# A gate left in PSUM and node one-hots made by eight comparisons, in a message-passing kernel on one core

## The chip, the core and the metric

The kernel runs on one core of a Trainium2 chip. A core has engines that run their own instruction queues side by side: TensorE (PE, with weight loads shown apart as PEld), VectorE (DVE), ScalarE (ACT), GpSimd (POOL) and SyncE (SP), and 16 DMA engines[...]. They meet through semaphores. The metric is the device time of one execution in microseconds, as the median of several runs. A separate execution is recorded by the hardware profiler, and everything that is said of single instructions comes from that one.

## What is computed

Four graph layers run over 6,250 nodes with 64 features and 206,250 edges that are sorted by their target node. The change lies in the third layer alone. Cut to what matters:

```python
h = relu(layernorm(x))
# third layer: V = h, E = edge_attr_64 (206250 x 64)
V  = leaky_relu(V, 0.2)
Vp = leaky_relu(V @ pAw + pAb, 0.2) @ pBw + pBb
e  = relu(relu(E @ mlp_w1 + mlp_b1) @ mlp_w2 + mlp_b2)
scale = sigmoid(e @ Bw + Bb)
shift = e @ Cw + Cb
msg  = scale * Vp[src] + shift
M    = clip(msg, 1e-5) ** 2
mean = segment_sum(M, dst) / max(count(dst), 1)
x    = x + sqrt(mean)
```

`scale` is called the gate below. The other three layers are sums over neighbours, which the kernel does as matmuls with a dense matrix of edge counts, A.

## The kernel before

The edges are padded to 202 groups of 1,024: 128 partitions times J = 8 edges. A loop of slots runs over the groups (`slot`, L1428 on). It is a software pipeline: slot i starts group i and works on later steps of groups i-1 to i-6. TensorE, ScalarE and VectorE run in the order in which the slot writes their instructions down, so the code's order is each engine's queue. POOL and SP are not bound to it: they run ahead as far as buffers allow.

What happens to a group:

- `loaded` brings the edge features in from HBM, started on SP.
- `fetched` (L1354) gathers the rows Vp[src] into the tile `v`, by eight indirect DMAs that POOL issues, one for each of a partition's eight edges. `v` has four buffers, so POOL can be up to four groups ahead of the instruction that reads `v`. The row numbers come from the tile `src_g`.
- `turned_edges`, `layer` and `evicted` transpose the features and apply the two small layers (PE and ACT).
- `gates_and_shifts` (L1376, L1380) makes gate and shift side by side in one PSUM tile, `p_bc`, 128 x 8 x 2 x 64. There is one such tile, so the next group's matmuls wait until this group's reader is done.
- `gated` (L1385) is the sigmoid on ScalarE.
- `clipped` (L1389 to L1391) is, on VectorE, gate times `v`, plus shift, and the maximum with 1e-5.
- `squared` (L1396, L1397) squares on ScalarE. The square goes on as three bf16 parts in `m3`, through L1452 (VectorE), L1453 (ScalarE) and L1464 (VectorE).
- `compared_nodes` (L1401) makes the one-hots `to` that say which of 128 target nodes each edge belongs to.
- `summed` (L1408) multiplies, for each of the eight edges of a partition, the one-hot by the message: eight matmuls with `to` as the weights.
- `added_to_nodes` (L1416, L1421, L1424) folds the three parts and adds them to the nodes.

Between these, the slot places pieces of two other jobs: `crossed` (L1260 on PE, L1266 on VectorE) compares blocks of A with their mirror images, and `partial` (L748, L1285) starts the last layer's sums. Both share a pair of PSUM buffers, `p_sum`. `finished` (L1323 on) runs when the last group of a column of blocks is done.

`prepared` builds what the loop needs, during an earlier stage: among it `lane` (L1124, each edge's target node modulo 128, as bf16) and `count` (L1131, 0 to 127, each repeated eight times).

Of the kernel before, what the change touches and what calls it, by code (L numbers as in the profile page):

```python
# [8 lines left out]
F32 = mybir.dt.float32  # L9
BF16 = mybir.dt.bfloat16  # L10
FP16 = mybir.dt.float16
I32 = mybir.dt.int32
AF = mybir.ActivationFunctionType
OP = mybir.AluOpType
AX = mybir.AxisListType

P = 128
N = 6250
D = 64
# [6 lines left out]
J = 8  # L26
G = -(-E // (P * J))
# [589 lines left out]
def fast(ctx, tc, bad, x, src, dst, edge_attr, W3, b3, W4, b4, w1, b1, w2, b2, Bw, Bb, Cw, Cb,  # L617
         pAw, pAb, pBw, pBb, out):

    nc = tc.nc  # L620
# [135 lines left out]
    with ExitStack() as ph:  # L756

        ipool = ph.enter_context(tc.tile_pool(name="ipool", bufs=1, reuse_waits="tile"))
        with ExitStack() as first:
# [9 lines left out]
                op0=OP.mult)  # L769
# [6 lines left out]
                                           op0=OP.mult, op1=OP.add)  # L776
# [9 lines left out]
        count = ipool.tile([P, 128, GQ], BF16, name="count")  # L786
# [14 lines left out]
        for c0, c1 in ((0, 3), (3, 10), (10, GC)):  # L801
            for c in range(c0, c1):
# [5 lines left out]
                                    op0=OP.mult, op1=OP.max)  # L808
# [21 lines left out]
        with ExitStack() as ps:  # L830
            psum = ps.enter_context(tc.tile_pool(name="ps0", bufs=1, space=PSUM, reuse_waits="tile"))
            p = psum.tile([P, SG, P], F32, name="p_a", bufs=2)
            nc.tensor.transpose(p[:D, 0, :], W3_sb, ident)
            nc.vector.tensor_copy(W3T, p[:D, 0, :])
            p = psum.tile([P, SG, P], F32, name="p_a", bufs=2)
# [34 lines left out]
            for c in range(GC):  # L870
# [6 lines left out]
                                        op0=OP.is_lt, op1=OP.add, accum_out=n)  # L877
                nc.vector.tensor_add(exact_i[:, c:c + 1], begin[:, c:c + 1], n)
            for c in range(GC):
# [6 lines left out]
                                        op0=OP.subtract)  # L886
                nc.scalar.activation(digits[:, 1, :], run[:, :, 1], AF.Copy)
                p = psum.tile([P, 1024], BF16, name="p_dig")
# [6 lines left out]
                if c % 9 == 8 or c == GC - 1:  # L895
                    c0 = c // 9 * 9
                    p = psum.tile([P, 512], F32, name="p_node")
                    for k in range(3):
# [4 lines left out]
                        for i in range(c0, c + 1):  # L903
# [11 lines left out]
                                    op=OP.add)  # L915
            by_col = ipool.tile([GC, P, 2], F32, name="by_col")
            p = psum.tile([P, 512], F32, name="p_node")
# [7 lines left out]
            p = psum.tile([P, 512], F32, name="p_node")  # L925
# [116 lines left out]
    def prepared(psum):  # L1042

        cpool = apart.enter_context(tc.tile_pool(name="cpool", bufs=1, side="right", reuse_waits="tile"))
# [35 lines left out]
        for i in range(4):  # L1080
# [5 lines left out]
            for j0 in range(0, J, 4):  # L1086
                p = psum.tile([P, 4, GH], F32, name="p_turn", bufs=2)
# [19 lines left out]
        for g in range(1, G + 1):  # L1107
            if g == G or window(g) != window(g0):
# [4 lines left out]
                                op=OP.subtract)  # L1113
# [6 lines left out]
                                op=OP.add)  # L1120
        yield

        nc.vector.tensor_scalar(dst_g, dst_g, P - 1, None, op0=OP.bitwise_and)
        lane = cpool.tile([P, G, J], BF16, name="lane")  # L1124
        nc.vector.tensor_copy(lane, dst_g)
        own = cpool.tile([P, P // QN, 2], F32, name="own")
        nc.vector.memset(own[:, :, 0], 0.0)
        for q in range(P // QN):
            nc.vector.memset(own[q * QN:(q + 1) * QN, :q + 1, 0], 1.0)
        nc.vector.tensor_scalar(own[:, :, 1], own[:, :, 0], -1.0, 1.0, op0=OP.mult, op1=OP.add)  # L1130
        count = cpool.tile([P, P, J], BF16, name="count")  # L1131
        nc.gpsimd.iota(count, pattern=[[1, P], [0, J]], base=0, channel_multiplier=0,
                       allow_small_or_imprecise_dtypes=True)

        before.close()
# [7 lines left out]
    with ExitStack() as ph:  # L1143
        wpool = ph.enter_context(tc.tile_pool(name="wpool", bufs=2, reuse_waits="tile"))
        values = []
        with tc.tile_pool(name="apool", bufs=7, reuse_waits="tile") as apool, \
                tc.tile_pool(name="ps1", bufs=1, space=PSUM, reuse_waits="tile") as psum:

            def convolved(c, z):
                add_whole(z, V3, c)  # L1150
                nc.vector.tensor_mul(z, z, over_features(norm0[:, blocks(c)]))
                nc.vector.tensor_add(z, z, over_blocks(b4_r, CB))
                nc.vector.tensor_add(X[:, blocks(c), :], X[:, blocks(c), :], z)
                h = wpool.tile([P, CB, D], F32, name="h")
                if c == 0:
                    values.append(of_nodes(node))
                normed_and_split(h, values[0], c, norm3)


            with tc.manual_schedule(engines={ET.PE, ET.DVE}):  # L1160
                gather(apool, wpool, psum, V3, convolved, (
                    step for steps in (hidden(NC - 1, wpool, psum), prepared(psum))
                    for step in steps))
# [50 lines left out]
    with ExitStack() as ph:  # L1214
        cpool, w1_d, w2_d, b1_c, b2_c, BC, BC_b, ones, src_g, lane, own, count = made.pop()
        mpool = ph.enter_context(tc.tile_pool(name="mpool", bufs=3, reuse_waits="tile"))
# [126 lines left out]
        of = [{} for _ in range(G)]  # L1343
# [37 lines left out]
                                     h2[:, q * P:(q + 1) * P], BC, start=False, stop=(k == 1))  # L1381

        def gated(g):
            gate = of[g]["gate"] = mpool.tile([P, J, D], F32, name="gate")
            nc.scalar.activation(gate, of[g]["p_bc"][:, :, 0, :], AF.Sigmoid)  # L1385

        def clipped(g):
            m = of[g]["m"] = mpool.tile([P, J, D], F32, name="m")
            nc.vector.tensor_mul(m, of[g].pop("gate"), of[g].pop("v"))  # L1389
            nc.vector.tensor_add(m, m, of[g].pop("p_bc")[:, :, 1, :])  # L1390
            nc.vector.tensor_scalar_max(m, m, EPS)  # L1391

        def squared(g):
# [3 lines left out]
            nc.scalar.activation(m, m, AF.Square)  # L1397

        def compared_nodes(g):
            to = of[g]["to"] = mpool.tile([P, P, J], BF16, name="to")  # L1400
            nc.vector.tensor_tensor(  # L1401
                to, count, lane[:, g, :].unsqueeze(1).to_broadcast([P, P, J]), op=OP.is_equal)

        def summed(g):
            p = of[g]["p_s"] = ps_a.tile([P, 512], F32, name="p_s")[:, :3 * D]
            m3, to = of[g].pop("m3"), of[g].pop("to")
            for j in range(J):
                nc.tensor.matmul(p, to[:, :, j], m3[:, j].rearrange("p t f -> p (t f)"),  # L1408
                                 start=(j == 0), stop=(j == J - 1))

        begun = set()
# [16 lines left out]
        def slot(i):  # L1428
# [7 lines left out]
            if at(M_AT):  # L1436
                gated(i - M_AT)
                clipped(i - M_AT)
# [10 lines left out]
            if at(M_AT):  # L1449
                compared_nodes(i - M_AT)  # L1450
                m, m3 = of[i - M_AT].pop("m"), of[i - M_AT]["m3"]
                nc.vector.tensor_sub(m, m, m3[:, :, 0, :])  # L1452
                nc.scalar.activation(m3[:, :, 1, :], m, AF.Copy)  # L1453
# [13 lines left out]
            if at(SUM_AT):  # L1467
                summed(i - SUM_AT)
# [28 lines left out]
    with ExitStack() as ph:  # L1497
# [5 lines left out]
        for layer in range(3):  # L1503
# [25 lines left out]
            else:  # L1529
                for s in range(CS):  # L1530
# [3 lines left out]
                    t = whole[:, :, s % 2 * CW:(s % 2 + 1) * CW]  # L1534
                    p = psum.tile([P, 512], F32, name="p_sum", bufs=2)
# [48 lines left out]
```

## Time and profile before

| what | value |
|---|---|
| timed runs, median of 3 | 4,146.01 us (4,139.06 to 4,147.82) |
| the profiled execution's own time | 3,611.97 us |
| its span, first to last instruction | 3,610.2 us |
| TensorE clock granted, mean | 0.904 |
| busy in the span: PE, PEld, DVE, ACT, POOL | 84%, 59%, 54%, 34%, 46% |
| gathers L1354, POOL | 1,616, busy 1,592.1 us |
| gate times v, L1389, DVE | 202, mean 694 ns |
| one-hots, L1401, DVE | 202, mean 687 ns |
| sigmoid, L1385, ACT | 202, mean 603 ns from 1,500 to 3,000 us |

The profile's page has the busy time of each engine, the span in slices, the chain of work that ended last, and groups of instructions by line with their mean duration and the idle time of the engine just before them. A trace can also be asked for the instructions of one line or tile, for the busy time in given stretches, and for the instructions in order of time. "PE busy" counts pipelined matmuls and is no measure of how near PE is to its limit. The timed runs are 534 us longer than the profiled execution, and the page shows only the latter.

### The profile page before, as it was taken

What the parts mean: (1) busy time and instruction counts of PE and PEld (TensorE: products, weight loads), DVE (VectorE), ACT (ScalarE), POOL (GpSimd) and SP (SyncE); (2) the same over time, 40 slices, a digit from 0 to 9 for tenths busy, and PEclk for the clock granted to TensorE, in tenths of its full rate; (3) what the DMA queues carried; (4) which work ended last, traced back from release to release, by engine and by line L of the source; (5) the groups of instructions that cost most, each with busy time, mean ns of one, the idle gap of its engine ahead of it and who ended that gap; (6) DMA issues with size and microseconds to landing.
All of it is one profiled execution on the core that took longest, in us unless ns stands there. A gap on an engine that the chain in (4) does not pass through costs nothing.

```text
span 3610.2 us, 59581 instructions
## 1 busy us (share of the span) xinstructions
PE 3039.4 (84%) x24393; PEld 2141.2 (59%) x24393; DVE 1954.2 (54%) x3899; ACT 1239.3 (34%) x2024; POOL 1665.0 (46%) x1889
## 2 busy tenths in 40 slices
PE   1699999999977777878878887878887888799999
PEld 0466667999954444444444444444454444489998
DVE  6899993532235546556555655655655565531111
ACT  1577772000023434434333443434433444210000
POOL 4200001000037777777777777777777777400000
PEclk9699999999988888889889888888988888799999
DMA  3233335565532223223323232322332322256664
GB/s 107 64 91 95 95 95 189 188 205 183 178 101 80 77 53 84 71 70 97 86 68 97 70 85 79 88 68 76 91 88 70 94 70 68 81 166 194 196 206 143
DMA packets 229312, 388.76 MB, mean 108 GB/s; under 512 B 137573, under 2 KB 139743, under 8 KB 228771
## 3 DMA queue, kind: packets, MB, share of 16 engines
q1 hardware_dynamic: 170420, 321.51, 28.3%
q0 software_dynamic: 55104, 60.65, 8.3%
q8 instruction: 193, 3.16, 0.4%
q10 hardware_dynamic: 3504, 2.70, 0.3%
q14 instruction: 91, 0.75, 0.1%
HBM read 340.47 MB, written 44.24 MB: 107 GB/s over the span
## 4 chain that ended last, share of the span: by engine, by line
POOL 35%; PE 35%; issue 14%; DMA 9%; DVE 5%; ACT 1%; POOLq 0%; DVEq 0%; SPq 0%; ACTq 0%
POOL v L1354 35%; PE p_acc L1026 21%; PE p_sum L748 7%; DMA v<-Vp_dram,src_g 7%; PE p_a L861 4%; DMA near<-pairs,begin_i 1%; PE p_node L739 1%; DMA piece<-A 1%; DVE lo L852 0%; DMA run<-pairs,exact_i 0%; PE p_acc L1023 0%; PE p_node L970 0%; PE p_bc L1380 0%; DMA X<-in_x 0%; PE p_node L975 0%
## 5 line engine op out<-in xcount | busy, mean ns | idle before, releaser
L1354 POOL DMA_INDIRECT v<-Vp_dram,src_g x1616 | 1592.1, 985 | 859.9 <-issue 828.6
L1026 PE MATMUL p_acc<-U,piece 128*128 128x192 bf16 x9604 | 817.7, 246 | 5.0 <-DMA piece<-A 5.0
L1026 PEld LDWEIGHTS <-piece 128*128 128x128 fp8e4 x9604 | 798.9, 98 | 17.0 <-DMA piece<-A 5.2
L1380 PE MATMUL p_bc<-BC,h 128*128 128x256 f32 x1616 | 585.8, 496 | 0.0
L1389 DVE TENSOR_TENSOR m<-gate,v 128x512 f32<-128x512 f32 x202 | 140.3, 694 | 762.5 <-DMA v<-Vp_dram,src_g 627.7
L1380 PEld LDWEIGHTS p_bc<-BC,h 128*128 128x128 f32 x1616 | 341.2, 234 | 154.7 <-issue 116.2
L1396 ACT ACTIVATE m<-m 128x512 bf16<-128x512 f32 x202 | 127.2, 630 | 821.9 <-DVE m L1391 821.9
L748 PEld LDWEIGHTS <-U 128*64 128x64 bf16 x4116 | 231.1, 112 | 215.4 <-issue 68.3
L1036 DVE TENSOR_REDUCE zg<-p_acc 128x128 f32<-128x384 f32 x112 | 56.3, 507 | 537.4 <-PE p_acc L1026 536.9
L865 ACT ACTIVATE strip<-p_a 128x784 fp8e4<-128x784 f32 x392 | 302.3, 820 | 112.6 <-PE p_a L861 112.0
L1376 PE MATMUL p_bc<-BC_b,ones 3*128 3x512 bf16 x404 | 180.9, 448 | 167.3 <-DVE m L1390 167.2
L1260 PE MATMUL p_sum<-ident_b,piece 128*128 128x128 bf16 x1372 | 154.9, 238 | 183.7 <-DVE junk L1266 183.4
L1260 PEld LDWEIGHTS <-piece 128*128 128x128 fp8e4 x1372 | 117.7, 107 | 318.8 <-issue 301.2
L1376 PEld LDWEIGHTS <-ones 3*128 3x128 bf16 x404 | 37.5, 93 | 439.4 <-DVE m L1390 235.3
L1366 PE MATMUL p<-h,w_d 128*128 128x512 f32 x404 | 253.5, 713 | 38.6 <-ACT h L1370 38.6
L748 PE MATMUL p_sum<-piece,U 128*64 128x448 fp8e4 x2058 | 238.1, 374 | 27.0 <-DVE junk L1266 18.7
L1370 ACT ACTIVATE h<-p,b_c 128x512 f32<-128x512 f32 x404 | 255.8, 684 | 12.9 <-PE p L1366 12.6
L1266 DVE SCALAR_TENSOR_TENSOR junk<-p_sum,there 128x512 bf16<-128x512 f32 (+1 forms) x392 | 242.1, 618 | 27.3 <-PE p_sum L1260 18.7
L748 PE MATMUL p_sum<-strip,U 128*64 128x448 fp8e4 x2058 | 242.0, 359 | 2.5 <-ACT U L711 1.4
L852 DVE TENSOR_TENSOR lo<-count,key 128x2048 bf16<-128x2048 bf16 x196 | 239.6, 1222 | 0.0
L861 PEld LDWEIGHTS <-lo 128*128 128x128 bf16 x3136 | 164.7, 103 | 98.6 <-DVE lo L852 75.8
L861 PE MATMUL p_a<-hd,lo 128*128 128x98 bf16 x3136 | 195.1, 217 | 32.6 <-DVE lo L852 31.1
(198 smaller groups left out, 3308.5 us busy)
## 6 DMA issues: line engine op xcount, KB each, us to landing
piece<-A SPq DMA_DIRECT2D x249, 784.0 KB, 4.3
e<-in_edge_attr SPq DMA_DIRECT2D x202, 256.0 KB, 2.7
A<-strip SPq DMA_DIRECT2D x14, 2744.0 KB, 13.1
v<-Vp_dram,src_g POOLq DMA_INDIRECT x1616
there<-A SPq DMA_DIRECT2D x28, 784.0 KB
pairs<-pair SPq DMA_DIRECT2D x1, 1616.0 KB, 5.3
Vp_dram<-v SPq DMA_DIRECT2D x7, 224.0 KB
out<-X SPq DMA_DIRECT2D x6, 224.0 KB
```

The source lines that it names most:

```text
L748: nc.tensor.matmul(p[half * D:(half + 1) * D, :w], U3[:, b, k, :], at_block, start=(i < 2), stop=(i >= 3 * n - 2))
L852: nc.vector.tensor_tensor(t, of.unsqueeze(1).to_broadcast(t.shape), key[:, k, at:at + GB].rearrange("p (h j) -> p h j", j=GQ) .unsqueeze(2 ...
L861: nc.tensor.matmul(p[:, j, :2 * NB], lo[:, g // GQ, :, g % GQ], hd[:, g // GQ, :, g % GQ], start=True, stop=True)
L865: nc.scalar.activation(strips[s][:, :, col:col + 2 * SG].rearrange("p b (j l) -> p b j l", l=2), p[:, :, :2 * NB].rearrange("p j (b l) -> ...
L1026: nc.tensor.matmul(p[d // 2][:, d % 2 * 3 * D:(d % 2 + 1) * 3 * D], t[:, b, d * P:(d + 1) * P], U3[:, k * CB + b, :, :].rearrange("p t f - ...
L1260: nc.tensor.matmul(p[:, a - a0, :], held["here", i, k][:, a, b * P:(b + 1) * P], ident_b, start=True, stop=True)
L1266: nc.vector.scalar_tensor_tensor(junk[:, :(a1 - a0) * P], p[:, :a1 - a0, :].rearrange("p a q -> p (a q)"), 15.5, of_there, op0=OP.min, op1 ...
L1354: nc.gpsimd.indirect_dma_start(out=v[:, j, :], out_offset=None, in_=Vp_dram[:, :], in_offset=bass.IndirectOffsetOnAxis(ap=src_g[:, g, j:j ...
L1366: nc.tensor.matmul(of[g][p], w, of[g].pop(x), start=True, stop=True)
L1370: nc.scalar.activation(of[g][t], of[g].pop(p), **how)
L1376: nc.tensor.matmul(p_bc[:, 4 * b:4 * b + 4].rearrange("p j o f -> p (j o f)"), ones, BC_b, start=True, stop=False)
L1380: nc.tensor.matmul(p_bc[:, 2 * q:2 * q + 2].rearrange("p j o f -> p (j o f)"), h2[:, q * P:(q + 1) * P], BC, start=False, stop=(k == 1))
```

## The change

Two things are done in the loop, with what they need in the preparation.

The sigmoid writes its result over its input in PSUM, into the first half of `p_bc`, and the multiply reads it from there. The SBUF tile `gate` is gone.

The one-hots are laid out edge by edge: `to` is now 128 x 8 x 128, so that the weights of one matmul lie side by side, where before they lay eight elements apart. One comparison of 1,024 elements between two tensors becomes eight comparisons of 128 elements, each of `count` with one value per partition. `count` needs no repeats any more (128 elements for 1,024), and `lane` is held as fp32.

```diff
-        lane = cpool.tile([P, G, J], BF16, name="lane")
+        lane = cpool.tile([P, G, J], F32, name="lane")
         nc.vector.tensor_copy(lane, dst_g)
...
-        count = cpool.tile([P, P, J], BF16, name="count")
-        nc.gpsimd.iota(count, pattern=[[1, P], [0, J]], base=0, channel_multiplier=0,
+        count = cpool.tile([P, P], BF16, name="count")
+        nc.gpsimd.iota(count, pattern=[[1, P]], base=0, channel_multiplier=0,
                        allow_small_or_imprecise_dtypes=True)
...
         def gated(g):
-            gate = of[g]["gate"] = mpool.tile([P, J, D], F32, name="gate")
-            nc.scalar.activation(gate, of[g]["p_bc"][:, :, 0, :], AF.Sigmoid)
+            gate = of[g]["p_bc"][:, :, 0, :]
+            nc.scalar.activation(gate, gate, AF.Sigmoid)
 
         def clipped(g):
             m = of[g]["m"] = mpool.tile([P, J, D], F32, name="m")
-            nc.vector.tensor_mul(m, of[g].pop("gate"), of[g].pop("v"))
-            nc.vector.tensor_add(m, m, of[g].pop("p_bc")[:, :, 1, :])
+            p_bc = of[g].pop("p_bc")
+            nc.vector.tensor_mul(m, p_bc[:, :, 0, :], of[g].pop("v"))
+            nc.vector.tensor_add(m, m, p_bc[:, :, 1, :])
             nc.vector.tensor_scalar_max(m, m, EPS)
...
         def compared_nodes(g):
-            to = of[g]["to"] = mpool.tile([P, P, J], BF16, name="to")
-            nc.vector.tensor_tensor(
-                to, count, lane[:, g, :].unsqueeze(1).to_broadcast([P, P, J]), op=OP.is_equal)
+            to = of[g]["to"] = mpool.tile([P, J, P], BF16, name="to")
+            for j in range(J):
+                nc.vector.tensor_scalar(to[:, j, :], count, lane[:, g, j:j + 1], None,
+                                        op0=OP.is_equal)
 
         def summed(g):
...
-                nc.tensor.matmul(p, to[:, :, j], m3[:, j].rearrange("p t f -> p (t f)"),
+                nc.tensor.matmul(p, to[:, j, :], m3[:, j].rearrange("p t f -> p (t f)"),
                                  start=(j == 0), stop=(j == J - 1))
```

The order of the instructions on every engine stays as it was, with eight comparisons in the one's place. No DMA is added, taken away or moved.

## The prediction, made before the changed kernel was run

> **What bounds the kernel now.** I first cut the span into stages at the first and last row gather of the messages. The columns are the stretch, then each engine's busy microseconds and instruction count, the granted TensorE clock, the DMA share and GB/s.
>
> ```profile
> core 0: us, PE busy (x) PEld busy (x) DVE busy (x) ACT busy (x) POOL busy (x), PEclk, DMA share, GB/s
> ...
> 560.00:1042.00 482.00, 454.84 (x5180) 433.18 (x5176) 157.50 (x292) 25.29 (x49) 18.32 (x215) 0.98 0.56 179
> 1042.00:3127.00 2085.00, 1670.35 (x8265) 968.21 (x8267) 1198.73 (x2701) 850.76 (x1448) 1592.06 (x1616) 0.86 0.30 80
> 3127.00:3200.00 73.00, 64.48 (x563) 40.85 (x560) 45.62 (x86) 13.18 (x22) 0.00 (x0) 0.92 0.39 134
> ```
>
> All that the change touches per group runs in the second stretch: 2,085 us, 58% of the span of 3,610.2. By busy share PE (80%) looks like the limit. The gathers' own rows say otherwise (least, middle and longest duration in ns; then what ended the idle time before them).
>
> ```profile
> L1354 POOL DMA_INDIRECT v<-Vp_dram,src_g x1616: 940/944/1476, 1041.9 to 3125.3; - x180
> ...
>   issue: 828.6, 1513
>   DMA v<-Vp_dram,src_g: 28.3, 93
> ...
>   DVE m L1389: 627.7, 156
> ```
>
> A gather takes 944 ns and the next starts 0.30 us later, without exception: 1,616 x (0.944 + 0.304) = 2,017 us, plus the excess of the mean (985 ns) over 944, 1,616 x 41 ns = 67 us, is 2,084 us, the stage. POOL never waits for a buffer. The last line says who waits: the first VectorE instruction of a group, L1389, waited 627.7 us for gathered rows in 156 of 202 groups, and 134.8 us for the gate in 46. So this stage is as long as the gathers, and the only part of it that other engines set is those 67 us. The timeline shows what they are (start, duration, engine).
>
> ```profile
> 1486.02 0.69 DVE L1389 TENSOR_TENSOR m<-gate,v 128x512 f32<-128x512 f32 x1 [4.68 <-DMA v<-Vp_dram,src_g]
> 1486.10 1.43 POOL L1354 DMA_INDIRECT v<-Vp_dram,src_g  x1 [0.30 <-issue]
> 1486.81 0.69 DVE L1390 TENSOR_TENSOR m<-m,p_bc 128x512 f32<-128x512 f32 x1
> ```
>
> ```profile
> 1478.05 0.69 DVE L1401 TENSOR_TENSOR to<-count,lane 128x1024 bf16<-128x1024 bf16 x1
> 1478.17 1.39 POOL L1354 DMA_INDIRECT v<-Vp_dram,src_g  x1 [0.30 <-issue]
> 1478.65 0.68 DVE L1452 TENSOR_TENSOR m<-m,m 128x512 f32<-128x512 f32 x1
> ```
>
> A gather that starts while L1389 or L1401 runs is longer by (that instruction's end - the gather's start - 0.13 us): 1486.02 + 0.69 - 1486.10 - 0.13 = 0.48, and 0.94 + 0.48 = 1.42. I laid all 1,616 gathers against the VectorE instruction running at their start. The rule accounts for nearly all of the 67 us: L1401 23.8 us (61 gathers), L1389 20.6 (81), L1464 8.8 (66), L1452 8.4 (36), the per-column node work some 4. L1390 and L1266, with one input in PSUM, delay none.
>
> [...] the four lines above have two SBUF inputs[...]. [...] L1391, fp32 from SBUF to SBUF with a constant, takes 426 ns, but up to 671 when it starts 0.52 to 0.75 us into a gather. If it starts 0.41 to 0.51 us into one, the gather ends up to 0.11 us late. [...] L900 (bf16, 1,152 columns) takes 472 ns and L1401 687 for 1,024[...].
>
> **The change part by part.**
>
> The multiply by the gate: the gate's input moves to PSUM, v stays in SBUF. It then has the form of L1390 (one SBUF, one PSUM input, 688 ns against 694), so its duration stays and its hold on gathers goes: -20.6 us. p_bc is released by the following add, as before, so the PE queue behind it sees no new wait. ScalarE now writes the sigmoid to PSUM with a stride. No row has that form; L1385 takes 603 ns into SBUF, the other evictions 579 to 684. I take no change. At +-0.1 us a group it lies in ScalarE's idle time (41% busy in the stage) and, in the 46 groups that wait for the gate, behind four groups of v buffers: cost 0.
>
> The one comparison: L1401 goes, and its hold with it: -23.8 us.
>
> The eight comparisons: the nearest rows are these.
>
> ```profile
> L1424 DVE TENSOR_SCALAR H<-r_s,own x49: 242/249/381, 1079.2 to 3101.7; 128x64 f32<-128x64 f32 x49
> ```
>
> L1424 has a per-partition operand[...]: 249 ns each. In the timeline an instruction without a wait starts 83 ns before its forerunner's recorded end, so eight take 8 x 166 = 1.33 us against 0.60 for L1401 (1478.05 to 1478.65): +0.73 us a group, +147 us of VectorE work. What hides it is the wait for rows and gate, 762.5 us or 3.8 us a group. Without this cover it would cost the whole 147.
>
> Their hold on gathers: a gather starting within one of them waits to its end less 0.13, so 122 ns of each can hurt, by 61 on average: 8 x 122/1249 x 61 = 48 ns a group, 202 x 48 = +10 us. [...] +18 if each gather caught waits half of 166 (202 x 1.06 x 83). [...] Conversely they wait for POOL by at most 0.25 us, within the same cover.
>
> What comes forward: when L1389 stopped a gather, it fixed the gathers' phase for the rest of the group. Without that, L1391, which now delays none, catches 300/1249 of the starts for 150 ns: 202 x 36 = +7 us (0 to 7). L1452 and L1464 cost 17.2 us now. At even phases L1452 would cost 563/1249 x 282 = 127 ns, 26 us in all, and L1464, which follows 1.39 us after it, about 14: +23 us at most; -17 if they slip clear. I take +11, half of the excess.
>
> PE: loading `to` with a 16-byte stride takes 145 ns, where L861's weights take 98. 8 x 47 = 0.38 us a group are saved off the path (the matmuls of L1408 follow at 82 ns[...]). The shorter index ramp and the float lane are one-time work before the stage, beside PE's p_acc: 0. No DMA moves, and nothing on SP's queue.
>
> Sum on the profiled execution: -20.6 - 23.8 + 10 + 7 + 11 = -16 us, from -61 (with -17 and no new holds) to +4 (18, 7 and 23). That execution took 3,611.97 us; the timed runs have a median of 4,146.01, 534 us more, which no view explains. I carry microseconds over unchanged: 4,130 us. Scaled by 1.15 it would be -18; if those 534 us mean that another engine is the limit there, 0.
>
> **Rivals.**
>
> Nothing to measure (the waits change place): all new holds at their even-phase value give -44.4 + 10 + 7 + 23 = -4 us; or the timed runs are not limited by the gathers. For it: the 67 us are few, and two of the four holders stay. Against: the two that cost most go. 4,146 us.
>
> Slower, by starvation: the burst of 1.33 us is longer than a gather's period of 1.249, so every group has a gather starting in it. [...] that gather waits for the rest of the burst, 0.65 us on average: 202 x 0.65 = +131, which takes the place of my +10, so -16 - 10 + 131 = +105, 4,251 us; with half the wait 4,186. It decides from a mean wait of 0.13 us a group (26 us / 202), where the sum's other terms are used up. Against: where two two-input instructions follow each other closely (L1401 and L1452, six gathers; L852's pairs), the gather slipped in at the first one's end. [...]
>
> Slower, by VectorE's queue: the next instruction behind the comparisons is L1452, and behind that L1464 (PE's sums) and L1266 (PE's crossings). If in the timed runs the 3.8 us of cover are not there, 0.73 us a group come onto the path: up to +147 - 44, 4,249 us. Against: no group's gather waited for VectorE in the profile.
>
> **How the numbers follow.** What a measurement of this kernel can tell from no change is about 0.2%, 8.3 us. Forecast 0.54, 4,085 to 4,150, with 0.48 of it over 8.3 us faster and 0.06 within; nothing to measure 0.16, of which 0.14 lies within and 0.02 beyond it faster; starvation 0.20; VectorE's queue 0.10. Faster 0.50, same 0.20, slower 0.30. The range, 4,088 to 4,190, leaves out the lowest end of the forecast and the upper half of both slower rivals, under 0.2 together.
>
> **What would show it.** The gathers' middle value stays at 944 ns and their mean falls from 985 to about 975 (16 us / 1,616). The multiply and the comparisons vanish as large holders; comparisons last about 249 ns at 166 ns apart, and delayed gathers end at a comparison's end. I am wrong if the mean gather rises (starvation), if L1389's successor begins to wait for the gate in most groups (VectorE's queue), or if the profile gains and the timed runs don't.

## The result, and the profile after

| | median | lowest to highest | runs |
|---|---|---|---|
| kernel before, beside it | 4,128.93 us | 4,103.59 to 4,153.84 | 20 |
| changed kernel | 4,133.61 us | 4,100.33 to 4,156.41 | 20 |

The ratio is 1.0009, with a 95% interval of 0.9988 to 1.003: no change that can be measured, where 16 us less were forecast. The profiled execution of the changed kernel took 4,148.39 us, its span is 4,146.6 us. So this profile shows what the profile before (3,610.2 us) did not: an execution as long as the timed ones. The stages of it come first (the stretch, then each engine's busy microseconds and instructions, TensorE clock, DMA share, GB/s), then the gathers, then the page's chain and two of its groups.

```profile
600.00:1047.00 447.00, 426.79 (x4911) 411.29 (x4908) 156.71 (x290) 23.68 (x46) 4.82 (x9) 0.99 0.54 169
1047.00:3640.00 2593.00, 1797.48 (x8139) 989.22 (x8140) 1317.14 (x4048) 852.12 (x1432) 1580.40 (x1616) 0.79 0.25 64
```

```profile
L1354 POOL DMA_INDIRECT v<-Vp_dram,src_g x1616: 939/944/1562, 1047.6 to 3638.1; - x180
its engine sat idle before it (us, times) until:
  issue: 820.6, 1441
  DVE m L1390: 534.8, 98
```

```profile
PE 51%; DVE 18%; another core or an unknown queue 12%; issue 9%; ACT 7%; DMA 2%; POOL 1%; DVEq 0%; SPq 0%; ACTq 0%; POOLq 0%
...
L1390 DVE TENSOR_TENSOR m<-p_bc,v 128x512 f32<-128x512 f32 x202 | 139.7, 692 | 613.9 <-ACT p_bc L1385 405.7
L1266 DVE SCALAR_TENSOR_TENSOR junk<-p_sum,there 128x512 bf16<-128x512 f32 (+1 forms) x392 | 242.7, 619 | 338.2 <-remote 210.2
```

The message stage is 2,593 us long, 508 more than before; the stage ahead of it is as fast as ever (clock 0.99). In it POOL now waits for buffers: 98 gathers stood 534.8 us until the multiply (L1390) freed a `v`. A gather itself takes 978 ns in the mean, 7 less than before. So what is longer is not the gathers; they have become the ones that wait. The chain of waits puts 1% on POOL and 12% on "another core or an unknown queue". One core runs, so that is a wait whose releaser the trace doesn't show. TensorE's clock in the stage is lower too (0.79, 0.86 before), but TensorE's busy time grew by only 127 of the 508 us. The timeline tells what the waits look like; VectorE first, then TensorE in the same stretch.

```profile
1513.35 0.43 DVE L1392 TENSOR_SCALAR m<-m 128x512 f32<-128x512 f32 x1
1516.91 0.69 DVE L1266 SCALAR_TENSOR_TENSOR junk<-p_sum,there 128x512 bf16<-128x512 f32 x1 [3.14 <-remote]
1517.53 0.08 DVE L1266 DVE_READ_ACCUMULATOR junk<-p_sum,there 128x1 f32 x1
1526.82 0.56 DVE L1266 SCALAR_TENSOR_TENSOR junk<-p_sum,there 128x384 bf16<-128x384 f32 x1 [9.21 <-remote]
```

```profile
1505.43 0.39 PE L1260 MATMUL p_sum<-ident_b,piece 128*128 128x128 bf16 x4
...
1507.61 0.33 PE L1260 MATMUL p_sum<-ident_b,piece 128*128 128x128 bf16 x3
1517.66 0.59 PE L1260 MATMUL p_sum<-ident_b,piece 128*128 128x128 bf16 x4 [9.72 <-DVE junk L1266]
```

The four-matmul block that the first L1266 reads was done at 1505.43 + 0.39 = 1505.82, the three-matmul block for the second at 1507.94. VectorE was free at 1513.78, yet the two began at 1516.91 and 1526.82. The records of the semaphores show TensorE's next increments only at 1511.26, at 1516.89 and from 1526.71 on; the two L1266 begin within 0.11 us of the last two. So the second signal is some 19 us late. Of the 963 increments of TensorE that are recorded between 1,047 and 3,100 us, some 400 came over 1 us behind the last TensorE instruction that could have made them; between 600 and 1,040 us, where no rows are gathered, none did. In the profile of before, none of 1,370 in the stage came over 0.02 us late. Many increments are missing from the records of after (963 for 1,083 instructions), so the exact lags are rough. In this execution signals between engines are late, and work that passes from engine to engine waits for them.

Two questions follow: whether the change made the signals late, and what it does where they aren't.

### The profile page after: what moved, and what is told of

Its sections match the earlier page's. It is cut to its first block, busy times and chain, and to the rows that moved or that the text cites. A ratio compares the mean times of both kernels' runs of the same rounds, so it can differ in the third digit from the quotient of the medians.

```text
span 4146.6 us, 60794 instructions
## 1 busy us (share of the span) xinstructions
PE 3184.1 (77%) x24393; PEld 2171.8 (52%) x24393; DVE 2092.3 (50%) x5313; ACT 1250.4 (30%) x2024; POOL 1652.5 (40%) x1889
## 4 chain that ended last, share of the span: by engine, by line
PE 51%; DVE 18%; another core or an unknown queue 12%; issue 9%; ACT 7%; DMA 2%; POOL 1%; DVEq 0%; SPq 0%; ACTq 0%; POOLq 0%
PE p_acc L1026 18%; PE p_sum L748 9%; PE p_bc L1380 7%; PE p L1366 5%; PE p_a L861 4%; DVE to L1403 3%; DVE junk L1266 2%; ACT h L1370 2%; DVE m L1390 2%; DVE m L1391 2%; PE p_s L1410 2%; PE p_bc L1376 2%; ACT p_bc L1385 1%; PE p_e L1362 1%
## 5 line engine op out<-in xcount | busy, mean ns | idle before, releaser
L1026 PEld LDWEIGHTS <-piece 128*128 128x128 fp8e4 x9604 | 799.0, 98 | 17.2 <-DMA piece<-A 5.4
L1390 DVE TENSOR_TENSOR m<-p_bc,v 128x512 f32<-128x512 f32 x202 | 139.7, 692 | 613.9 <-ACT p_bc L1385 405.7
L1266 DVE SCALAR_TENSOR_TENSOR junk<-p_sum,there 128x512 bf16<-128x512 f32 (+1 forms) x392 | 242.7, 619 | 338.2 <-remote 210.2
L748 PE MATMUL p_sum<-piece,U 128*64 128x448 fp8e4 x2058 | 270.0, 386 | 99.2 <-issue 68.6
L1366 PE MATMUL p<-h,w_d 128*128 128x512 f32 x404 | 277.1, 768 | 72.4 <-ACT h L1370 52.6
L1410 PE MATMUL p_s<-m,to 128*128 128x192 bf16 x1616 | 206.1, 279 | 132.1 <-issue 63.9
L1455 ACT ACTIVATE m<-m 128x512 bf16<-128x512 f32 x202 | 127.2, 630 | 584.9 <-DVE m L1454 358.1
L1403 DVE TENSOR_SCALAR to<-count,lane 128x128 bf16<-128x128 bf16 x1616 | 289.6, 273 | 0.0
L1366 PE MATMUL p<-eT,w_d 128*128 128x512 f32 x404 | 245.7, 693 | 11.0 <-ACT h L1370 9.0
L1410 PEld LDWEIGHTS <-to 128*128 128x128 bf16 x1616 | 160.4, 111 | 167.2 <-issue 155.2
L1397 ACT ACTIVATE m<-m 128x512 bf16<-128x512 f32 x202 | 127.2, 630 | 395.1 <-DVE m L1392 246.5
```

The lines of the kernel that those rows point to most:

```text
L748: nc.tensor.matmul(p[half * D:(half + 1) * D, :w], U3[:, b, k, :], at_block, start=(i < 2), stop=(i >= 3 * n - 2))
L1026: nc.tensor.matmul(p[d // 2][:, d % 2 * 3 * D:(d % 2 + 1) * 3 * D], t[:, b, d * P:(d + 1) * P], U3[:, k * CB + b, :, :].rearrange("p t f - ...
L1266: nc.vector.scalar_tensor_tensor(junk[:, :(a1 - a0) * P], p[:, :a1 - a0, :].rearrange("p a q -> p (a q)"), 15.5, of_there, op0=OP.min, op1 ...
L1366: nc.tensor.matmul(of[g][p], w, of[g].pop(x), start=True, stop=True)
L1403: nc.vector.tensor_scalar(to[:, j, :], count, lane[:, g, j:j + 1], None, op0=OP.is_equal)
L1410: nc.tensor.matmul(p, to[:, j, :], m3[:, j].rearrange("p t f -> p (t f)"), start=(j == 0), stop=(j == J - 1))
```

## The experiments

Twelve kernels were run, in four sets; each set has its own runs of the kernel before, on the same chip, and each set ran on another chip. A chip is called of the short kind where the kernel before took near 3,610 us, and of the long kind where it took near 4,130 or more. Line numbers move by one to seven with the edits. In the text I name the instructions: the multiply, the comparisons, and the two subtractions that split the message (L1452 and L1464 before).

### The kernel before, again

No edit.

> The kernel before, unchanged, recorded once more. The profile of after shows signals between engines that arrive 1 to 19 us late in the message stage; the first profile of before shows almost none and is 534 us shorter than its timed runs. Theory A (the late signals belong to the usual execution of either kernel, and the first profile of before is the exception): this profile has a span of 4,100 to 4,150 us, a message stage near 2,590 us and gathers that wait 400 to 600 us for L1389. Theory B (the change brought the late signals in, and the 534 us of before lie elsewhere): a span near 3,610 us, or a long one whose gathers never wait for L1389.

3,610.34 us, beside 3,607.99 for the same kernel in the set; ratio 1.0003 (0.9995 to 1.0012).

```profile
L1354 POOL DMA_INDIRECT v<-Vp_dram,src_g x1616: 940/947/1465, 1042.6 to 3129.1; - x180
its engine sat idle before it (us, times) until:
  issue: 825.6, 1503
  DMA v<-Vp_dram,src_g: 30.8, 101
```

On this chip the timed runs take what the profile of before showed, POOL waits for no buffer, and no recorded increment of TensorE in the stage is late. Theory A as put falls: late signals don't belong to the kernel's timed runs everywhere. Theory B's number came, but since the timed runs beside it are as short, it doesn't speak for its cause either. The 534 us are a difference between one set of runs and another. Each chip was used in one set only, so a property of the chip can't be told from its state at that time; the record doesn't say on which chip the first profile of before was taken. The next two sets fell on chips of the short kind too, the last on one of the long kind.

### The gathers left out

This kernel leaves out the row gathers and loads other rows of the same size in their place, so it computes something else.

```diff
-            for j in range(J):
-                nc.gpsimd.indirect_dma_start(
-                    out=v[:, j, :], out_offset=None, in_=Vp_dram[:, :],
-                    in_offset=bass.IndirectOffsetOnAxis(ap=src_g[:, g, j:j + 1], axis=0))
+            r = g % 6 * P * J
+            nc.sync.dma_start(v, Vp_dram[r:r + P * J, :].rearrange("(p j) f -> p j f", j=J))
```

> The kernel before with the row gathers left out: each group's v is loaded by one plain transfer of consecutive rows on SP's queue, so the third layer's messages are computed from other rows. Theory C (the signals are late because of the gathers that GpSimd issues): the late signals go, the stage is set by PE and the chain of a group, 1,700 to 1,900 us, and the whole takes 3,250 to 3,450 us. Rival (the lateness has another source): the whole stays above 3,800 us, since even without gathers the group's chain is as slow as in the profile of after.

3,132.61 us, ratio 0.8685 (0.8671 to 0.87), with TensorE's clock at 0.974. The chain of waits:

```profile
PE 58%; DVE 21%; ACT 16%; DMA 3%; issue 2%; POOL 0%; DVEq 0%; SPq 0%; ACTq 0%; POOLq 0%
```

Under the gathers lies a kernel that is some 475 us shorter, below the 3,250 to 3,450 us that were expected. So on this chip the gathers are the bound, with much room beneath them. Theory C was about late signals; this chip had none to lose, so the run says nothing on it.

### Either half of the change alone

The gate in PSUM with the one comparison of before, and the eight comparisons with the gate in SBUF (the halves of the diff above).

> Only the gate's half of the change: sigmoid written over its input in PSUM, multiply reads it there. Prediction's theory (the gathers set the stage, holds on them count): 0.5% faster at most, -20 us. Theory A (gathers wait for the group's chain anyway, so freed gathers gain nothing): no change, 0.997 to 1.003, with fewer delayed gathers in the profile and the same stage.

> Only the one-hots' half of the change: eight comparisons with a per-partition operand, gate in SBUF as before. Prediction's theory: -14 us (holds of the one comparison go, smaller ones come), the 147 us of added VectorE work hidden. Theory A with VectorE on the group's chain: slower by up to 147 us (ratio up to 1.035); with the chain's waits absorbing it, 1.000 to 1.005.

Gate alone: 3,606.10 us, ratio 0.9998 (0.9989 to 1.0006), no change, where the prediction's sum gave 20 us less. Comparisons alone: 3,612.79 us, ratio 1.0013 (1.0006 to 1.002), so 5 us slower rather than faster. Where did the freed microseconds go? As for the prediction, I call what a gather takes over 944 ns a hold, and put it down to the VectorE instruction that ran some 0.1 us after the gather's recorded start (us, and in brackets the gathers caught). The last column is the changed kernel, which the next section shows:

| holder | before, again | gate alone | comparisons alone | both |
|---|---|---|---|---|
| multiply | 20.9 (80) | - | 22.0 (87) | - |
| comparison(s) | 26.0 (62) | 25.9 (71) | 1.4 (73) | 1.0 (61) |
| first subtraction | 7.0 (36) | 12.8 (50) | 28.3 (69) | 31.0 (82) |
| second subtraction | 8.9 (68) | 9.6 (72) | 15.8 (122) | 14.7 (109) |
| all holders | 67.5 | 58.2 | 72.3 | 57.3 |

Each half does remove its own hold. With the single comparison gone, the first subtraction holds four times as much as before.

### The changed kernel on a chip of the short kind

> The changed kernel as it is, beside the kernel before, on whatever chip comes. Theory C (the waits change place): what the multiply and the single comparison gave up is taken back by the two subtractions behind them, so where the kernel before takes near 3,608 us this one takes 3,600 to 3,612, ratio 0.998 to 1.001, gathers 975 to 985 ns in the mean. Theory D (the prediction's sum holds where gathers bind, and only the other chip hid it): 16 us faster, ratio near 0.9955, gathers near 975. Theory E (the changed kernel itself makes signals late and the clock low, as in its first profile): near 4,130 us here too, with the multiply's buffer holding POOL up in about 100 places.

3,608.97 us against 3,611.69, ratio 0.9996 (0.9988 to 1.0005). The gathers:

```profile
L1354 POOL DMA_INDIRECT v<-Vp_dram,src_g x1616: 940/944/1534, 1042.7 to 3116.3; - x180
...
  issue: 829.5, 1516
...
who waited for it (us, times):
  DVE m L1390: 535.7, 144
```

Theory E is out: POOL waits for no buffer, VectorE waits for rows as before, and none of TensorE's 1,373 recorded increments in the stage came over 0.02 us late. Theory D's 16 us didn't come; the changed kernel gains at most 4 us here, and the gathers' mean is 979 ns, both as theory C had it. This is one of the holds that took the multiply's place:

```profile
2887.88 1.40 DVE L1403 TENSOR_SCALAR to<-count,lane 128x128 bf16<-128x128 bf16 x8
2887.91 0.94 POOL L1354 DMA_INDIRECT v<-Vp_dram,src_g  x1 [0.30 <-issue]
...
2889.16 1.53 POOL L1354 DMA_INDIRECT v<-Vp_dram,src_g  x1 [0.30 <-issue]
2889.20 0.68 DVE L1454 TENSOR_TENSOR m<-m,m 128x512 f32<-128x512 f32 x1
```

The gather that lies within the eight comparisons takes its 0.94 us. The next is recorded as starting 40 ns ahead of the first subtraction, and lasts until 0.81 us after that has ended, as in the prediction's rule; the last comparison ended 0.6 us sooner, so it isn't what held the gather.

Why just there? In 144 of 202 groups the multiply is released by the landing of a gathered row, so much of what follows it stands at similar distances from the gathers in many groups. 71 of the 202 multiplies start 250 to 375 ns after a gather's start; evenly spread it would be 20. The comparisons last some 0.7 us longer than the one before, and put the first subtraction's start into the last 125 ns ahead of a gather, the worst place, in 42 groups. With the comparisons alone it was there in 39 groups, with the gate alone in 6, and in the kernel before once. So it is the longer comparisons that move it there.

### Subtractions with a PSUM input

If two-SBUF-input instructions are what holds the gathers, the remedy is to leave none. The gate's half of `p_bc` is free once the multiply is done, so the square can be written there, and the first subtraction has one input in PSUM. In the second version its difference stays there as well, and both have.

```diff
-            nc.scalar.activation(m, m, AF.Square)
+            sq = of[g]["sq"] = of[g].pop("p_bc")[:, :, 0, :]
+            nc.scalar.activation(sq, m, AF.Square)
...
-                nc.vector.tensor_sub(m, m, m3[:, :, 0, :])
+                nc.vector.tensor_sub(m, of[i - M_AT].pop("sq"), m3[:, :, 0, :])
```

> The changed kernel with the fp32 square written into the gate's place in PSUM, so that the first subtraction behind the comparisons has one SBUF and one PSUM input. Theory C in its strict form (a hold that goes is taken back by the next holder): the first subtraction's holds go (about 20 to 25 us in the runs so far), the second one's grow, and the time stays within 5 us of the changed kernel. Theory F (holds simply add): 15 to 25 us faster than the changed kernel where the gathers bind. A third way: p_bc, of which there is one, is released about 2.5 us later in each group, and TensorE's next gate matmuls wait; if that is not covered, up to 2.5 x 202 = 505 us slower.

> As the one before, and the first difference stays in PSUM as well, so that both subtractions have a PSUM input and no VectorE instruction of a group is left that has two SBUF inputs, apart from the crossings. Theory F and theory C agree: nothing is left that could take a hold over, so the gathers' mean falls to 944 to 955 ns and the stage to about 2,017 to 2,035 us, 30 to 50 us under the kernel before where the gathers bind. If instead the gate matmuls' wait for p_bc (now about 3.7 us later than before) is not covered, slower by up to 3.7 x 202 = 750 us.

One subtraction: 3,573.94 us, ratio 0.9901 (0.9886 to 0.9916), 35 us under the changed kernel on the same chip. Its hold is gone, and the second subtraction holds 9.2 us, less than the 14.7 in the changed kernel: the strict form of theory C is out, holds can also fall together. All holders have 22 us left of 57.3, so the holds fell by the same 35 us as the time. That is more than theory F's 15 to 25, which had put the first subtraction's hold at 20 to 25 us where it was 31. Both: 3,791.51 us, ratio 1.0507 (1.0492 to 1.0521). The gathers and their waits, the multiply's, and those behind the second subtraction, in this last kernel:

```profile
L1354 POOL DMA_INDIRECT v<-Vp_dram,src_g x1616: 940/947/1208, 1042.3 to 3275.3; - x180
its engine sat idle before it (us, times) until:
...
  DVE m L1390: 235.6, 127
```

```profile
  ACT p_bc L1385: 788.1, 186
```

```profile
  PE p_bc L1376: 467.1, 185
  PEld L1376: 305.6, 91
```

The holds went as expected (16.6 us in all), but there is one `p_bc`. It now comes free only after the second subtraction, TensorE's gate matmuls wait for it, the multiply waits 788.1 us for the gate, and at last POOL waits for the multiply. Of the two outcomes expected this is the slower one: 2,233 us of stage / 202 = 11.05 us a group, against 9.99 for eight gathers.

### Comparisons done twice

```diff
+            to2 = mpool.tile([P, J, P], BF16, name="to2")
+            for j in range(J):
+                nc.vector.tensor_scalar(to2[:, j, :], count, lane[:, g, j:j + 1], None,
+                                        op0=OP.is_equal)
```

> The changed kernel with its eight comparisons done twice, the first time into a tile that nothing reads: 1.33 us more of VectorE work in each group, 269 us in all. If VectorE's work is covered by the wait for rows, the time stays within 10 us of the changed kernel (0 for the work, up to +10 for holds). If VectorE's queue is the limit it rises by 150 to 269 us; the half-way case, 30 to 100 us, says that part of the groups has no cover.

3,626.5 us, ratio 1.004 (1.0027 to 1.0054): 17.5 us over the changed kernel, outside the first expectation and under the others.

```profile
L1354 POOL DMA_INDIRECT v<-Vp_dram,src_g x1616: 940/947/1551, 1043.1 to 3136.9; - x180
...
who waited for it (us, times):
  DVE m L1390: 307.8, 112
```

The multiply's wait for rows fell from 535.7 to 307.8 us: that much of the added 269 us went into the cover. The holds rose from 57.3 to 75.1 us, by 17.8, which is the time lost, and of it the comparisons, all sixteen, have 4.5 us. The rest lies with the instructions around them: 2.9 us more with the first subtraction, 5.2 with the second, and 5.6 with the gathers that start during the add or the maximum behind the multiply.

### The square in PSUM without the change, and the comparisons moved ahead

The first of these is the kernel before with the PSUM square alone. The other two are the PSUM versions with the eight comparisons moved ahead of the multiply, where VectorE waits for rows:

```diff
                 gated(i - M_AT)
+                compared_nodes(i - M_AT)
                 clipped(i - M_AT)
...
-                compared_nodes(i - M_AT)
```

> The kernel before (gate in SBUF, one comparison) with the fp32 square written into p_bc, so that the first subtraction has a PSUM input. If a line's hold is worth what the trace shows of it, the gain is the 7 to 9 us that the first subtraction cost there: ratio near 0.998. If the holder next in the queue takes over what is freed, 0: ratio near 1. If the square in PSUM brings the 1% of the run before by something else than holds (an earlier or later release of buffers, TensorE's stretches), about 35 us here too: ratio near 0.990.

> Both subtractions with PSUM inputs, and the eight comparisons moved ahead of the gate's multiply, into the wait for rows. The loop over the one p_bc, which set 11.05 us a group (2,233 us / 202) when the comparisons lay inside it, is shorter by their 1.33 us: 9.7 us, under the gathers' 9.99. Theory F then gives a stage of 2,020 to 2,040 us and 3,550 to 3,575 us in all where the kernel before takes 3,610. If the loop over p_bc is longer than I count (groups that wait for the gate still set the pace), 3,600 to 3,700.

> One subtraction with a PSUM input and the comparisons ahead of the multiply. No buffer's loop is near the gathers' pace, so only the positions of the two-SBUF-input instructions against the gathers' starts move. If holds were the same at every position, 3,574 us as without the move; since the second subtraction now starts 1.33 us sooner after the rows' landing, it meets other starts, and theory C allows 3,565 to 3,590.

| kernel | ratio to before | gather, mean ns | all holders, us |
|---|---|---|---|
| before, square in PSUM | 0.9983 (0.9975 to 0.999) | 980 | 59.4 |
| changed, one subtraction in PSUM, comparisons first | 0.992 (0.9907 to 0.9934) | 969 | 38.5 |
| changed, both in PSUM, comparisons first | 0.9864 (0.9849 to 0.9879) | 950 | 11.1 |

The same edit that brings 35 us on the changed kernel brings 6.6 on the one before: there the first subtraction held only 7 to 9 us, and the single comparison (33.1 us) still stands. So on these chips the change is worth nothing by itself, and most of the gain came only with it. Whether one half of it would do wasn't run.

All three times lie where the expectations had them. Moving the comparisons ahead adds holds where a holder is left: the second subtraction went from 9.2 to 24.9 us by its new place. The time went from 3,573.94 to 3,584.34 us, but in different sets, and the intervals of the ratios overlap (0.9886 to 0.9916 and 0.9907 to 0.9934), so a loss of time is likely and not shown. Where no such holder is left the move is right, since it takes 1.33 us out of the loop over `p_bc`. That kernel took 3,563.2 us, 49 us less than the kernel before, the best of all.

The holds also account for the times. In all eight edited kernels whose stage the gathers set, the timed difference from the kernel before in the same set lies within 8 us of the difference in holds from the 67.5 of before: from +15 and +8 us for the doubled comparisons to -49 and -56 for this last kernel.

```profile
L1354 POOL DMA_INDIRECT v<-Vp_dram,src_g x1616: 940/944/1306, 1043.2 to 3070.3; - x180
```

```profile
  ACT p_bc L1385: 424.9, 174
  DMA v<-Vp_dram,src_g: 81.7, 28
```

From first to last gather it is 2,027 us, against 2,017 for 1,616 gathers without any hold. The second view is what the multiply waits for: the gate in 174 groups, the rows in 28. So VectorE rarely waits for rows any more, and the wait that hid added VectorE work is nearly used up.

### One more holder, on a chip of the long kind

```diff
+            to2 = mpool.tile([P, P, J], BF16, name="to2")
+            nc.vector.tensor_tensor(
+                to2, count, lane[:, g, :].unsqueeze(1).to_broadcast([P, P, J]), op=OP.is_equal)
```

> The kernel before with its one comparison done twice, the first time into a tile that nothing reads: one holder more on VectorE's queue, 0.69 us long like the one whose holds cost 24 to 26 us. Holds that add: 24 us slower, ratio near 1.0066. If what counts is where the queue's two-SBUF-input instructions lie against the gathers' starts, a gather caught by the pair is let in at the first one's end, and the added 0.6 us moves the two subtractions to other starts: anything from -10 to +35 us, with the subtractions' holds changed by more than 5 us. VectorE's queue itself stays covered in both: the multiply's wait for rows falls by about 202 x 0.6 = 121 us and nothing else.

4,184.02 us, beside 4,162.97 for the kernel before: ratio 1.0053 (1.0031 to 1.0074). The ratio is near what adding holds would give, but the profile says that it can't be read so: three lines of its page, which is of an execution of 4,224.84 us.

```profile
PE 49%; DVE 18%; another core or an unknown queue 13%; issue 10%; ACT 8%; DMA 2%; POOL 0%; DVEq 0%; SPq 0%; ACTq 0%; POOLq 0%
...
L1354 POOL DMA_INDIRECT v<-Vp_dram,src_g x1616 | 1603.8, 992 | 1435.6 <-issue 816.1
...
L1266 DVE SCALAR_TENSOR_TENSOR junk<-p_sum,there 128x512 bf16<-128x512 f32 (+1 forms) x392 | 241.7, 617 | 485.9 <-remote 347.9
```

All that marked the profile of the result is here, in a kernel that has nothing of the change: 13% without a releaser, L1266 waiting 485.9 us (26.3 in the changed kernel on a chip of the short kind), and POOL waiting 594.8 us for the multiply, in 85 gathers. TensorE's increments are late here as there, by up to 18 us. This answers the first question: the late signals come with the chip, or its state at the time, and not with the change. Where POOL waits for the multiply, VectorE's time can't be fully covered: 0.6 us more in a group, 121 us in all, went with 13 to 31 us. How much of that is VectorE's time and how much is holds, this run doesn't tell. The question that this run was made for, whether a holder added to the kernel before costs its own hold, stays open.

## Why the prediction was right or wrong, step by step

**The bound.** Right on chips of the short kind: the stage there is the gathers and their holds, in every kernel but the one whose `p_bc` loop is longer. In the runs of the result it was wrong: POOL is 1% of the chain, and its gathers wait. The prediction had said that 534 us were unexplained, that it carried its microseconds over all the same, and that 0 follows if another engine is the limit there. That last clause is the one that held.

**The multiply and the single comparison.** Both right: the holds of 20.6 and 23.8 us are gone wherever the edit was made and a profile taken. The sigmoid into PSUM costs nothing, 605 ns in the middle against 602. The multiply takes 692 ns with one PSUM input, 693 without.

**The eight comparisons.** Their price, an estimate taken over from L1424's 249 ns, was right: 249 ns in the middle, though the mean is 277, up to 498, and eight take 1.30 to 1.57 us rather than 1.33. Their hold was put too high: 1.0 us, where 10 were taken from 0 to 18. Of the gathers that start during a comparison, 61 were caught, by 16 ns in the mean. The other way round the price does rise: in the profile of the result all 107 comparisons that took over 400 ns started 0.47 to 0.63 us into a gather. That a burst keeps a gather out until its end was the supposition of the starvation rival (+105); with the small hold it falls. The rival on VectorE's queue also falls where the gathers bind: even twice the comparisons are covered.

**What comes forward.** The maximum behind the add (L1392 after) was put at +7 and holds 4.3 us. The step that failed is the re-phasing of the two subtractions: +11, at most +23, taken as half of what they would cost at even phases. They cost 31.0 + 14.7 = 45.7 us instead of 17.2, so +28. Even phases were the wrong upper bound, because the phases are not even: in 144 of 202 groups the multiply starts when a gather lands, and what stands behind it tends to keep its distance to the gathers. The prediction saw that the multiply's hold had fixed the phase; it missed that the landing fixes it too.

**The sum.** With the measured terms in the prediction's own sum: -20.6 - 23.8 + 1.0 + 4.3 + 28.5 = -10.6 us; the trace of the changed kernel gives 57.3 us of holds against 67.0, the same -10. The timed runs give -3, from -4 to +2. One profiled execution is a draw from those runs: the changed kernel's took 3,604.6, the lowest of its 13, and the one of before in the repeat 3,616.0 with a median of 3,610.3. By each kernel's distance from its median, 4 and 6 us, most of the difference between these two profiles is chance. A step of 10 us in this kernel can't be read from one profile of each.

**The result itself** is the rival "nothing to measure", which the prediction gave by two ways: the waits change place, or the timed runs are not limited by the gathers. Both are true, on different chips. The measured 4,133.61 us lies in the range of 4,088 to 4,190, and only 4 us from the 4,130 forecast, but this nearness is luck. The 4,130 was 16 us less than 4,146, a median of three executions; with 20 the kernel before has 4,128.93. The starting point was 17 us too high, and that hides the gain that didn't come. And the range was wide enough to hold no change, to which the prediction gave 0.20.

On the long kind the change adds 0.73 us a group to VectorE where such time is partly exposed; at the share that the doubled comparison lost on such a chip (21 of 121 us, taken as VectorE's time alone) an estimate is some 26 us. The measured difference is +5, from -5 to +12, so either the estimate is too high or something gives most of it back. Which, isn't known; no part of the change was run alone there. Nor was the best kernel run there.

Of the signs that the prediction named, the gathers' middle stayed at 944, and their mean fell to 979 and 978 instead of 975. The last of the signs of being wrong came true: the profile gained and the timed runs didn't.

## What to carry to other kernels

Taking away one instruction that holds an engine up doesn't always give its hold back. Here 44 us of holds went and some 3 us of time came, since other instructions took most of them over. So look where the next holder now falls, above all if the held engine's own result sets the rhythm. Look at the two-input VectorE instructions as a set, and move one input of each to PSUM where a half-used tile is at hand (35 us for the first subtraction of the changed kernel, 6.6 us in the kernel before), but count how long that tile is then kept (with both subtractions moved, ratio 1.0507). If the profiled execution and the timed ones differ by 14%, settle which of them the result will be measured in before adding up tens of microseconds.

## What was not expected of the hardware

The kernel before took 3,608 to 3,612 us on three chips, and 4,129 and 4,163 us in the two other sets of runs. Each of these two has one profile, and both show late signals, with a mean TensorE clock of 0.86 and 0.85 against 0.90 to 0.91 in the profiles of before and after on the short chips. In them semaphore increments came up to 18 or 19 us after their instruction's end, almost only in stretches in which rows are gathered. What makes them late wasn't found; leaving the gathers out was not tried on such a chip.

On the chip of the short kind VectorE's 128-element bf16 comparisons held the 61 gathers that they caught for 16 ns in the mean, while single comparisons took up to 498 ns instead of 249. In the profile of the result all 107 that took over 400 ns started 0.47 to 0.63 us into a gather.

Loading one-hots as weights fell from 145 to 98 ns when they became contiguous, as estimated. No gain in time came with it: the comparisons alone, which include it, were 5 us slower.
